# No chunk brought row by row, 311 counted chunks, three late node tiles, and other prices in the instruction planner of a two-layer graph kernel

## The chip, the core and the metric

The kernel runs on one core of a Trainium2 chip. TensorE (PE) multiplies matrices, VectorE (DVE) and ScalarE (ACT) work on elements, GpSimd (POOL) issues the indirect DMAs that gather rows by index, and SyncE (SP) issues most other DMAs; ScalarE issues some. The metric is the device time of one execution in microseconds. Differences below about 0.2% (2.5 us) are not told apart from no change.

## The reference

Two graph layers over N = 6250 nodes and E = 100000 edges sorted by target node `dst`, each an aggregation and a two-layer perceptron, then a residual layer norm (256 features in and out, 512 hidden):

```
def _gin_agg(h, src, dst, eps, n):
    return (1.0 + eps) * h + segment_sum(h[src], dst, n)
h = _gin_agg(x, src, dst, eps1, n)
h = relu(relu(h @ W1a + b1a) @ W1b + b1b)
h = _gin_agg(h, src, dst, eps2, n)
out = relu(h @ W2a + b2a) @ W2b + b2b
return layernorm(x + out)
# dst = min(6250 * uniform ** 2, 49999): low node numbers have many edges
```

The time goes into the two segment sums: 100000 rows of 256 floats in layer 1, 100000 rows of 512 floats in layer 2.

## The kernel before, in words

The nodes form 49 tiles of 128. The edges form 782 chunks of 128. A chunk's contribution to its targets is computed in one of two ways.

**Counted chunks** are the first 308, whose targets lie in the 8 heavy node tiles. For each chunk VectorE makes a one-hot of the source within its tile times all 49 tiles (`cb`, line 1923), ScalarE the one of the source's low part (`ca`, line 1902), PE multiplies them (line 1954) and VectorE adds the product into node-by-node counts (`upper_counts`, `lower_counts`, line 2181). The counts are used as a dense matrix: in layer 1 by `first_products` (line 1831), in layer 2 by `second_products` (line 1712), which multiplies the counts (`cf`, a float copy made by ScalarE at line 1639 of the bytes `ci` that SP loads at line 1621) with the layer-1 result of a range of nodes, split in two parts (`upper`, `xr`). The second products for the first ranges (those whose layer-1 nodes are done) run already in layer 1.

**Gathered chunks** are the others. GpSimd fetches 128 rows with one indirect DMA (line 527) into `early`, in layer 2 in turn with `late`, a tile in memory that layer 1 uses until its last second product. There is room for 24 gathers (PIECES = 6 pieces of BURST = 4). PE sums them by a one-hot of the targets (`sel`, line 1207), 2 pieces in a turn in layer 1 and 3 in layer 2; the sums are merged (lines 1258, 1262, 1278) and added by VectorE to the node tiles (line 1287).

A **dense block** then takes two node tiles: transposes (line 1331), first weights (line 1400), second weights (line 1433), and in layer 1 the bias and ReLU (lines 1446, 1449) and the store of `h1r` to DRAM (line 1450, on ScalarE's DMA queue); in layer 2 the layer norm and the output DMA (line 1496, on SP's). The layer-1 blocks of the last nodes end in the order of tiles ..., 11 and 10, 12, 9, 7, 8.

**Ferried chunks**: for five groups of layer 1 the group's last chunk isn't gathered by GpSimd. SP reads its 128 source indices into registers and issues 128 DMAs of one row (line 2217) into `b2b_c`, 640 in all, and one matmul for each (line 1219) sums it. When the last is summed `b2b_c` gets its own data, a bias (line 2221).

**Early gathers** (`fore`): gathers of layer 2 read the layer-1 result, so they wait for its stores. Two groups of 12 chunks each (FORES) go first and read only nodes below the LATE tiles (7 and 8), whose indices are replaced by a row of zeros; what the edges from the LATE tiles add comes later, by one-hot products of those tiles' own results: VectorE makes 24 one-hots over LATE's nodes (line 1113) and PE multiplies them.

Instructions are written in an order that is fixed before the kernel runs. A planner (class `Plan`) runs all steps as processes on a clock of its own, with a price in `yield ("on", engine, price, rank)`, rooms for the buffers, rests, and due times (GATHERS for a gather, LANDINGS, SUMS and TURN for the sums, PATIENT for the loads and casts of the ranges of the second products, HASTE for the layer-2 start). Its clock fixes only the order in each engine's queue; on the chip, semaphores decide when something runs. A different price therefore moves instructions in a queue without changing them.

Of the kernel before, what the change touches and what calls it, by code (L numbers as in the profile page):

```python
# [11 lines left out]
I32 = mybir.dt.int32  # L12
# [33 lines left out]
SIGMAS = 4.0  # L46
WIDTH = 4.5
# [44 lines left out]
def counted(N, E, tiles):  # L92
# [8 lines left out]
    while (  # L101
        node((total + PARTS) * P) < tiles * P
        and span(N, E, (total + PARTS) * P, P, SIGMAS) <= W
    ):
        total += PARTS
    k = -(-N // P)
    best = [(0.0, 0, 0)]
    for c in range(1, total + 1):
        found = []
        for n in range(1, min(c, LONGEST) + 1):  # L110
            w = min(math.ceil(span(N, E, c * P, n * P, WIDTH)), W)
            if span(N, E, c * P, n * P, SIGMAS) <= w:
# [87 lines left out]
GATHERS = (1.28, 1.265)  # L200
# [8 lines left out]
SUMS = 0.0021  # L209
TURN = (0.08, 0.2)  # L210
# [167 lines left out]
def tile_gin_residual_layernorm(  # L378
# [56 lines left out]
    NCP = groups[-1][0] + PARTS * groups[-1][1]  # L435
    runs = []
# [51 lines left out]
    ferries, t, free = [], FIRST, FERRY[0]  # L488
    for g in orders[1]:
        n = len(members[g])  # L490
        t += GATHERS[0] * n
        ready = free + FERRY[1] * P / FERRY[3] + FERRY[2]
        if ready <= t + LANDINGS[0] and t < FERRY[4] and members[g][-1][0] < full:
            ferries.append(g)
            t -= GATHERS[0]
            free = t + LANDINGS[0] + FERRY[2]
# [4 lines left out]
            for chunks in [members[g][: -1 if number == 1 and g in ferries else None]]  # L501
# [8 lines left out]
    fore = const.tile([P, FOREN], I32, name="fore")  # L510

# [35 lines left out]
    near = b1b_s = start = lowest = highest = ferried_from = None  # L547
# [280 lines left out]
    def ordered(ctx):  # L828
# [45 lines left out]
        def layer(number, pools, table, width, scale, weights, ba, wide, at=None, aside=None, right=None):  # L874
# [63 lines left out]
            sel_many = Tiles(keep, [P, GRP, SLOTS], F32, "sel", 2)  # L938
            to_room = Tiles(keep, [P, 2, P], F32R, "to", 4 if once else 5)
# [92 lines left out]
            def scaling(b, token):  # L1032
# [3 lines left out]
                yield ("on", "ACT", act(len(ts) * width), 2)  # L1036
# [42 lines left out]
            def late_edges(g):  # L1079
# [20 lines left out]
                assert len(hot) >= n  # L1100
# [10 lines left out]
                for i, (c, part) in enumerate(members[g]):  # L1111
                    yield ("on", "DVE", 0.22, 1)
                    nc.vector.tensor_scalar(
                        hot[i], numbers[:, : T * P], spot[:, c - c0 : c - c0 + 1], None,
                        op0=ALU.is_equal,
                    )
                assert n == PARTS * h
                yield ("on", "PE", 0.3 + 0.04 * n, 1)
                for i, (c, part) in enumerate(members[g]):
                    nc.tensor.matmul(  # L1120
                        ap[part * SLOTS : (part + 1) * SLOTS, : T * P], sel[:, c - c0, :], hot[i],
                        start=(i < PARTS), stop=(i >= n - PARTS),
                    )
# [50 lines left out]
            def sums():  # L1174
# [7 lines left out]
                while i < len(pieces[number]):  # L1182
# [4 lines left out]
                    for i in some:  # L1187
                        yield ("until", selected[pieces[number][i][0]])
                        yield ("until", arrived[i])
                        if once and i == last[pieces[1][i][0]] and pieces[1][i][0] in ferries:  # L1190
                            yield ("until", ferried[pieces[1][i][0]])
# [5 lines left out]
                    for i in some:  # L1197
# [18 lines left out]
                        if once and i == last[g] and g in ferries:  # L1216
# [3 lines left out]
                                pm[b * SLOTS : (b + 1) * SLOTS], sel[:, c - groups[g][0], :], b2b_c,  # L1220
# [21 lines left out]
            def merge(gs, shared):  # L1242
# [4 lines left out]
                yield ("on", "ACT", act(n * width), 0)  # L1247
# [35 lines left out]
                for i, (g, to, used, _) in enumerate(gs):  # L1283
                    for t in reach(g):
                        yield ("until", ready[t])
                        yield ("on", "DVE", dve(width), 1)
# [7 lines left out]
            def dense(b):  # L1294
# [98 lines left out]
                for o in range(0, KH, at_once):  # L1393
# [12 lines left out]
                    def hidden(token=token, fs=fs, todo=todo):  # L1406
                        for f in fs:
                            yield ("on", "ACT", act(nb), 1)
# [1149 lines left out]
```

## Time and profile before

| | before |
|---|---|
| median of 3 runs | 1265.28 us (1265.19 to 1265.89) |
| profiled execution | 1263.54 us, span 1261.8 us |
| mean granted TensorE clock | 0.974 |
| busy PE / DVE / ACT / POOL | 1173.7 (93%) / 832.2 (66%) / 653.5 (52%) / 908.6 (72%) us |
| gathers of layer 1, early ones, rest of layer 2 | 469, 24, 450 |

The profiled execution is 1.74 us longer than its span. POOL's busy 72% hides that an indirect DMA shows 0.95 us of work and 0.30 us of issue before the next one starts. L followed by a number is a line of the kernel before, and an engine's name with a q (ACTq, SPq) is its DMA issue. One matmul of 32-bit data in the program leaves two records on PE, so x16 in a PE row is 8 matmuls of the program.

### The profile page before, as it was taken

The page shows a single profiled execution, that of the slowest core. Times are in us where ns is not written, and L with a number is a line of the kernel's source. Part 1 is how long each engine was busy: PE and PEld are TensorE (multiplying, and loading weights), DVE is VectorE, ACT ScalarE, POOL GpSimd, SP SyncE. Part 2 cuts the span into 40 slices and gives each one's busy share as a digit, 9 for nine tenths or more (in the row PEclk, how much of TensorE's full clock was granted, in tenths as well). Part 3 has the DMA queues.
Part 4 walks back from the last instruction along what each step waited for, and adds up shares of the span by engine and source line. Part 5 has one row for each costly group of instructions (what it writes and reads, how often), then busy time and mean ns, then how long its engine had stood idle before and what let it go on. Part 6 is the DMA issues. An engine that isn't in the chain of part 4 may idle for free. (4 is left out here: it accounts for less than half of the span.)

```text
span 1261.8 us, 21174 instructions
## 1 busy us (share of the span) xinstructions
PE 1173.7 (93%) x6204; PEld 775.9 (61%) x6204; DVE 832.2 (66%) x2123; ACT 653.5 (52%) x1367; POOL 908.6 (72%) x956
## 2 busy tenths in 40 slices
PE   5879998999999999989979999998998999999998
PEld 4445455655555666556646767665766767777667
DVE  7899998888878743334356768676875565555243
ACT  7656678898896674534443633432533344321222
POOL 6777777777777777777267777777777777777760
PEclk9799999999999999989989999999998999999899
DMA  6445467666547776665388888888888888877871
GB/s 213 139 138 156 128 185 215 190 205 191 156 143 205 228 221 205 213 193 164 112 290 297 302 263 254 277 304 278 282 274 276 289 261 295 252 212 235 252 220 40
DMA packets 137652, 276.06 MB, mean 219 GB/s; under 512 B 21757, under 2 KB 68680, under 8 KB 137532
## 3 DMA queue, kind: packets, MB, share of 16 engines
q0 software_dynamic: 60432, 185.79, 48.0%
q1 hardware_dynamic: 43012, 56.43, 13.5%
q10 hardware_dynamic: 34088, 32.43, 8.0%
q8 instruction: 52, 0.85, 0.3%
q14 instruction: 68, 0.56, 0.2%
HBM read 248.95 MB, written 25.62 MB: 218 GB/s over the span
## 5 line engine op out<-in xcount | busy, mean ns | idle before, releaser
L527 POOL DMA_INDIRECT early<-in_x_dram,srcs x469 | 450.9, 961 | 146.3 <-issue 126.2
L527 POOL DMA_INDIRECT early<-h,places x226 | 216.4, 958 | 68.9 <-issue 54.5
L527 POOL DMA_INDIRECT late<-h,places x224 | 216.1, 965 | 68.2 <-issue 57.6
L1287 DVE SCALAR_TENSOR_TENSOR acc<-bank,mask,acc 128x256 f32<-128x256 f32 (+1 forms) x352 | 201.3, 603 | 59.1 <-PE bank L1278 57.2
L1433 PE MATMUL bank<-w1b_s,ht 128*128 128x512 f32 (+1 forms) x392 | 183.7, 595 | 0.4 <-ACT ht L1410 0.4
L1712 PE MATMUL bank<-upper,cf 128*128 128x512 f32 (+1 forms) x392 | 171.2, 437 | 8.7 <-ACT cf L1639 4.6
L1712 PE MATMUL bank<-xr,cf 128*128 128x512 f32 (+1 forms) x392 | 158.4, 404 | 2.7 <-DVE xr L1600 2.7
L1400 PE MATMUL bank<-zt,w2a_s 128*128 128x256 f32 (+2 forms) x736 | 152.0, 360 | 0.7 <-ACT zt L1359 0.7
L1400 PEld LDWEIGHTS bank<-zt,w2a_s 128*128 128x128 f32 x736 | 128.9, 192 | 25.5 <-issue 3.3
L1207 PE MATMUL bank<-early,sel 128*32 128x256 f32 (+1 forms) x1414 | 124.7, 467 | 18.9 <-DMA early<-h,places 6.2
L1639 ACT CAST cf<-ci 128x512 fp32r<-128x512 uint8 (+1 forms) x104 | 60.9, 594 | 154.3 <-PE bank L1712 113.5
L1657 DVE TENSOR_TENSOR whole_acc<-bank,whole_acc 128x512 f32<-128x512 f32 x96 | 65.1, 683 | 86.0 <-PE bank L1712 86.0
L1061 DVE TENSOR_TENSOR sel<-iota,slot 128x256 f32<-128x256 f32 (+2 forms) x112 | 49.0, 437 | 95.6 <-PE bank L1207 91.9
L1831 PE MATMUL bank<-cf,xh 128*128 128x512 f32 x392 | 108.8, 418 | 1.7 <-DVE xh L1770 1.5
L1902 ACT ACTIVATE ca<-numbers,low 128x128 f16<-128x128 f16 x308 | 98.1, 391 | 21.8 <-PE bank L1954 20.0
L1433 PEld LDWEIGHTS bank<-w1b_s,ht 128*128 128x128 f32 (+1 forms) x392 | 71.6, 190 | 60.6 <-issue 52.9
L1278 PE MATMUL bank<-split,to 128*128 128x512 f32 (+2 forms) x332 | 92.4, 397 | 15.4 <-ACT split L1258 7.6
L1410 ACT ACTIVATE ht<-bank,b2a_s 128x256 f32<-128x256 f32 (+2 forms) x92 | 37.1, 446 | 130.4 <-PE bank L1400 130.4
L1400 PE MATMUL bank<-zt,w1a_s 128*128 128x256 f32 (+2 forms) x432 | 97.2, 371 | 4.8 <-ACT zt L1359 3.8
L1258 ACT CAST split<-bank 128x512 fp32r<-128x512 f32 (+1 forms) x111 | 63.6, 583 | 66.3 <-PE bank L1207 53.1
L1712 PEld LDWEIGHTS bank<-upper,cf 128*128 128x128 f32 (+1 forms) x392 | 75.3, 192 | 33.1 <-ACT upper L1595 5.8
L1207 PEld LDWEIGHTS bank<-early,sel 128*32 128x32 f32 x1414 | 38.3, 110 | 91.1 <-issue 45.5
(203 smaller groups left out, 1870.6 us busy)
## 6 DMA issues: line engine op xcount, KB each, us to landing
raw<-in_x_dram ACTq DMA_DIRECT2D x48, 256.0 KB
h<-h1r ACTq DMA_DIRECT2D x48, 256.0 KB
b2b_c<-in_x_dram SPq DMA_DIRECT2D x640, 1.0 KB
xr<-h SPq DMA_DIRECT2D x10, 1024.0 KB
acc<-h SPq DMA_DIRECT2D x17, 512.0 KB
early<-in_x_dram,srcs POOLq DMA_INDIRECT x469
ci<-counts SPq DMA_DIRECT2D x24, 256.0 KB
acc<-in_x_dram SPq DMA_DIRECT2D x21, 256.0 KB
```

Of the source, the lines that this page charges most:

```text
L527: nc.gpsimd.indirect_dma_start(out=rows_[:, j, :], out_offset=None, in_=table, in_offset=bass.IndirectOffsetOnAxis(ap=rows_in[:, c - first ...
L1207: mm = nc.tensor.matmul(pm[b * SLOTS : (b + 1) * SLOTS], sel[:, c - groups[g][0], :], rows_[:, l, :], start=(c == part[0]), stop=(c == par ...
L1258: nc.scalar.copy(to_ if parted else to_.bitcast(F32), ap[:used, at_])
L1278: nc.tensor.matmul(pu[:, at_], lhs, rhs, start=(l == 0), stop=(l == 1 or not parted),)
L1287: nc.vector.scalar_tensor_tensor(acc[t], pu[:, i * width : (i + 1) * width], mask[:, t - lo[g], g : g + 1], acc[t], op0=ALU.mult, op1=ALU.add,
L1400: nc.tensor.matmul(ph[:, (f - o) * TILES * P : (f - o) * TILES * P + nb], wa[:, k, f * P : (f + 1) * P], zt[:, k, :nb], start=(k == 0), st ...
L1433: nc.tensor.matmul(po[:m], ht[:, f, i * P : i * P + m], wb[:, f, :], start=(f == 0), stop=(f == KH - 1),)
L1639: nc.scalar.copy(cf_token.tile[:, : n * P].rearrange("p (k j) -> p k j", j=P), token.tile[:, :n, a : a + P],)
L1657: nc.vector.tensor_tensor(sums_of[t], bank[token.number][:, :width], sums_of[t], op=ALU.add)
L1712: nc.tensor.matmul(bank[token.number][:, :width], cf[:m, j * P : (j + 1) * P], of[:m, j, :], start=(j == 0 and of is upper), stop=(j == le ...
L1831: nc.tensor.matmul(bank[tokens[f].number][:, :c], xh[:m, j, l, f * P : (f + 1) * P], cf[:m, :c], start=(k == 0 and l == 0), stop=(k == NT ...
L1902: nc.scalar.activation(token.tile[:, j, :], numbers[:, :P], AF.Abs, bias=low[:, q * BATCH + j : q * BATCH + j + 1],)
```

## The change

No chunk is ferried any more in layer 1; the code can now ferry in layer 2 too, but the limits in FERRY (-10 and -90) let no group through in either layer. The number of counted chunks no longer rises in steps of PARTS and may exceed the window's width by OVER = 0.1, which makes it 311. So layer 1 has 471 gathers (469 before: 5 ferried ones come back, 3 become counted) and layer 2 has 24 early and 447 others (450). LATE covers tiles 7 to 9, so the one-hots of the early groups' late part are 384 wide (256 before) and are made in two halves; FORES becomes the next lower two groups, over two node tiles that are set `apart` instead of three. A number of prices and due times is changed. The rest of the diff changes the code of ferrying, for rows that are not used here.

```
-PATIENT = 16.0
+PATIENT = (16.0, 16.0, 9.0)
-FERRY = (45.0, 5.6, 5.0, 8, 610.0)
+FERRY = ((45.0, 0.7, 5.0, -10.0, 1), (4.0, 0.52, 6.0, -90.0, 1))
-LATE = (7, 9)
-HASTE = -20.0
+LATE = (7, 10)
+HASTE = -23.0
...
-    while (
-        node((total + PARTS) * P) < tiles * P
-        and span(N, E, (total + PARTS) * P, P, SIGMAS) <= W
-    ):
-        total += PARTS
+    while node((total + 1) * P) < tiles * P and span(N, E, (total + 1) * P, P, SIGMAS) < W + OVER:
+        total += 1
...
-GATHERS = (1.28, 1.265)
+GATHERS = (1.262, 1.262)
...
-SUMS = 0.0021
-TURN = (0.08, 0.2)
+SUMS = 0.00168
+TURN = (0.12, 0.12)
...
+                for o in range(0, n, turn_):
+                    some = list(enumerate(members[g]))[o : o + turn_]
+                    for i, (c, part) in some:
+                        yield ("on", "DVE", 0.1 + 0.0005 * T * P, 1)
+                        nc.vector.tensor_scalar(
+                            hot[i - o], numbers[:, : T * P], spot[:, c - c0 : c - c0 + 1], None,
+                            op0=ALU.is_equal,
+                        )
...
-                    yield ("on", "PE", 0.14 * kk * len(some), 2)
+                    yield ("on", "PE", 0.11 * kk * len(some), 2)
...
-                            yield ("on", "DVE", (2 if soon else 3) * dve(D) + 0.2, 2)
+                            yield ("on", "DVE", (1.03 if soon else 1.49), 2)
...
-                            yield ("on", "PE", 2 * PASS * len(ks) * width, first or 3)
+                            yield ("on", "PE", 0.2 + 2 * PASS * len(ks) * width, first or 3)
...
-                            cost += 0.16 + 0.00027 * NT * width_of[c]
+                            cost += 0.125 + 0.00027 * NT * width_of[c]
...
-                yield ("on", "DVE", 0.2 + 0.00106 * NT * w, 1)
+                yield ("on", "DVE", 0.08 + 0.00106 * NT * w, 1)
...
-                nc.sync.dma_start(b2b_c, b2b.partition_broadcast(P))
...
+                if once:
+                    for i in range(len(mine), len(ferries[2])):
+                        edges_in(from2, 2, i)
+                    for g in mine:
+                        yield ("until", landed[g])
+                    nc.sync.dma_start(b2b_c, b2b.partition_broadcast(P))
```

SP's queue late in layer 1, before. A row is a line, what is issued and its shape; `b2b_c` is the ferry's tile, `ferried_from` its indices, `ci_8014` the count bytes of one half of the heavy tiles for a range, `xr` that range's layer-1 result.

```order
L2217 DMA b2b_c<-in_x_dram 1x256
L1621 DMA ci_8014<-counts 128x2048
L2211 TENSOR_LOAD ferried_from
L2217 ISA
...
L1518 DMA xr<-h_60 128x4x512
L1621 DMA ci_8107<-counts 128x2048
L1621 DMA ci_8178<-counts 128x2048
L1518 DMA xr<-h_60 128x4x512
L2221 DMA b2b_c<-in_L_gnn_b2b_dram 128x256
```

The same place after the change:

```order
L1529 DMA acc_5744<-h_60 128x2x512
L1634 DMA ci_5782<-counts 128x2048
L1529 DMA acc_5800<-h_60 128x2x512
L1634 DMA ci_6002<-counts 128x2048
L1529 DMA xr<-h_60 128x4x512
L1634 DMA ci_6076<-counts 128x2048
L1634 DMA ci_6160<-counts 128x2048
```

Ahead of and behind each load of count bytes there were row loads of the ferry; now only other loads of the second products and of the seeds stand there.

GpSimd's gathers at the seam of the two layers, before:

```order
L527 DMA early<-in_x_dram,srcs 128x256 x469
L527 DMA early<-h_60,fore 128x512 x12
L527 DMA late<-h_60,fore 128x512 x12
L527 DMA early<-h_60,places_72 128x512 x10
```

After the change:

```order
L535 DMA early<-in_x_dram,srcs 128x256 x471
L535 DMA early<-h_60,fore 128x512 x12
L535 DMA late<-h_60,fore 128x512 x12
L535 DMA early<-h_60,places_72 128x512 x11
```

Two gathers more stand ahead of the early ones; the order and number of the early ones are the same.

TensorE from the last sum of layer 2 (line 1207 before, 1217 after) on, before:

```order
L1207 MATMUL bank_95<-late,sel 32x512 x4
L1433 MATMUL bank_92<-w2b_s,ht 128x256 x2
L1400 MATMUL bank_98<-zt,w2a_s 128x128 x8
L1278 MATMUL bank_91<-split,to 128x512 x2
...
L1331 MATMUL bank_94<-ident,whole_acc 128x128 x4
L1433 MATMUL bank_93<-w2b_s,ht 128x256 x2
L1331 MATMUL bank_97<-ident,apart 128x128 x4
L1400 MATMUL bank_95<-xr,w2a_s 128x128 x8
L1433 MATMUL bank_93<-w2b_s,ht 128x256 x2
```

After the change:

```order
L1217 MATMUL bank_98<-late,sel 32x512 x4
L1444 MATMUL bank_97<-w2b_s,ht 128x256 x2
L1342 MATMUL bank_99<-ident,acc_10424 128x128 x4
L1289 MATMUL bank_93<-split,to 128x512 x2
L1411 MATMUL bank_95<-zt,w2a_s 128x128 x8
L1342 MATMUL bank_96<-ident,whole_acc 128x128 x4
L1411 MATMUL bank_94<-zt,w2a_s 128x128 x8
L1342 MATMUL bank_92<-ident,apart 128x128 x4
L1411 MATMUL bank_98<-xr,w2a_s 128x128 x8
```

Behind the last sum to the end stand, before, 8 blocks of first weights (8 matmuls each), 10 of second weights (2 each), 12 transposes and 2 merge matmuls; after, 6, 7, 12 and 2.

## Rows read from the trace of the kernel before

**Rows 1.** Timeline of POOL: start, length, engine, line, tile, count, idle before and releaser.
```profile
599.09 0.94 POOL L527 DMA_INDIRECT early<-in_x_dram,srcs  x1 [0.30 <-issue]
...
621.27 0.94 POOL L527 DMA_INDIRECT early<-h,fore  x1 [21.24 <-PE bank L1400]
...
640.69 1.33 POOL L527 DMA_INDIRECT late<-h,fore  x1 [4.72 <-issue]
...
656.16 0.95 POOL L527 DMA_INDIRECT early<-h,places  x1 [0.30 <-PE bank L1207]
...
1224.34 1.12 POOL L527 DMA_INDIRECT late<-h,places  x1 [0.30 <-issue]
```

**Rows 2.** Groups of POOL: count, busy us, mean ns, idle before and its releasers.
```profile
L527 POOL DMA_INDIRECT early<-h,places x226 | 216.4, 958 | 68.9 <-issue 54.5 <-DMA early<-h,places 6.1 <-DMA late<-h,places 1.8
L527 POOL DMA_INDIRECT late<-h,places x224 | 216.1, 965 | 68.2 <-issue 57.6 <-DMA late<-h,places 5.2 <-PE bank L1712 1.5
```

**Rows 3.** Busy time in two stretches: PE, PEld, DVE, ACT, POOL, clock, DMA.
```profile
100.00:150.00 50.00, 44.44 (x227) 25.44 (x226) 46.43 (x120) 31.79 (x75) 38.11 (x40) 0.97 0.49 148
600.00:640.00 40.00, 38.87 (x189) 26.53 (x187) 12.58 (x22) 15.15 (x29) 11.38 (x13) 1.00 0.42 136
```

**Rows 4.** Timeline of ACT's DMA queue and PE at the seam.
```profile
601.74 0.33 ACTq L1450 DMA_DIRECT2D h<-h1r  x1
...
617.39 0.33 ACTq L1450 DMA_DIRECT2D h<-h1r  x1
...
633.76 0.39 PE L1712 MATMUL bank<-upper,cf 128*128 128x512 f32 x1
...
639.56 0.39 PE L1712 MATMUL bank<-xr,cf 128*128 128x512 f32 x1
```

**Rows 5.** Timeline of SP's queue, ACT and PE around 554 us.
```profile
523.88 26.47 SPq L2217 DMA_DIRECT2D b2b_c<-in_x_dram  x40
...
532.89 0.30 ACT L1639 CAST cf<-ci 128x128 fp32r<-128x128 uint8 x1 [1.62 <-PE bank L1712]
...
550.45 0.36 SPq L1621 DMA_DIRECT2D ci<-counts  x1
...
553.92 2.17 ACT L1639 CAST cf<-ci 128x512 fp32r<-128x512 uint8 x4 [10.85 <-DMA ci<-counts]
...
554.60 0.79 PE L1712 MATMUL bank<-upper,cf 128*128 128x512 f32 x1 [4.55 <-ACT cf L1639]
```

**Rows 6.** Groups of VectorE at the widest count step.
```profile
L2181 DVE TENSOR_TENSOR upper_counts<-bank,upper_counts 128x490 f32 x45 | 29.6, 659 | 2.4 <-PE bank L1954 1.9
L1923 DVE TENSOR_SCALAR cb<-numbers,si 128x490 f16<-128x490 f16 x78 | 25.6, 367 | 1.1 <-PE bank L1954 1.1
```

**Rows 7.** Timeline of VectorE and POOL at the late one-hots.
```profile
659.50 3.30 DVE L1113 TENSOR_SCALAR ht<-numbers,zt 128x256 f16<-128x256 f16 x16
...
662.61 1.02 POOL L527 DMA_INDIRECT early<-h,places  x1 [0.30 <-issue]
```

**Rows 8.** Timeline of PE from the last sum to the end.
```profile
1229.66 1.07 PE L1207 MATMUL bank<-late,sel 128*32 128x512 f32 x8 [1.76 <-DMA late<-h,places]
...
1242.69 1.95 PE L1400 MATMUL bank<-xr,w2a_s 128*128 128x128 f32 x16
1244.48 1.95 PE L1400 MATMUL bank<-zt,w2a_s 128*128 128x128 f32 x16
...
1253.73 1.89 PE L1433 MATMUL bank<-w2b_s,ht 128*128 128x256 f32 x8
```

**Rows 9.** Waits of PE from 640 us on: total us, times, longest.
```profile
PE bank L1207 <- DMA late<-h,places: 7.0, 3, 3.0
PE bank L1207 <- DMA early<-h,places: 6.2, 4, 4.1
```

**Rows 10.** Timeline of POOL and PE: a turn's first gather, and its sum.
```profile
1064.43 0.95 POOL L527 DMA_INDIRECT late<-h,places  x1 [0.30 <-PE bank L1712]
...
1081.94 2.78 PE L1207 MATMUL bank<-late,sel 128*32 128x512 f32 x24
```

More of the change, by code (lines that the diff above doesn't have):

```diff
@@ L435, in tile_gin_residual_layernorm @@
     NCP = groups[-1][0] + PARTS * groups[-1][1]
+    MOST = max(h for c, h in groups) * PARTS
     runs = []
@@ L487, in tile_gin_residual_layernorm @@
     orders[2] = FORES + [g for g in reversed(range(BEGIN[1], NG)) if g not in FORES]
[L488 to L496, printed above, removed]
+    ferries = {}
+    for number, order in orders.items():
+        begin, pace, landing, until, rooms_ = FERRY[number - 1]
+        t, sp, free, found = (FIRST, HASTE)[number - 1], begin, [begin] * rooms_, []
+        for g in order:
+            t += GATHERS[number - 1] * len(members[g])
+            ready = max(sp, free[len(found) % rooms_]) + pace * P + landing
+            if (
+                ready <= t + LANDINGS[number - 1] and t < until and members[g][-1][0] < full
+                and (number == 1 or g not in FORES)
+            ):
+                t -= GATHERS[number - 1]
+                sp = ready - landing
+                free[len(found) % rooms_] = t + LANDINGS[number - 1] + landing
+                found.append(g)
+        ferries[number] = found
     pieces = {
@@ L500, in tile_gin_residual_layernorm @@
             for g in order
-            for chunks in [members[g][: -1 if number == 1 and g in ferries else None]]
+            for chunks in [members[g][: -1 if g in ferries[number] else None]]
             for i in range(0, len(chunks), BURST)
@@ L546, in tile_gin_residual_layernorm @@
     flag = const.tile([1, 1], I32, name="flag")
-    near = b1b_s = start = lowest = highest = ferried_from = None
+    near = b1b_s = start = lowest = highest = ferried_from = ferried_to = None
     e1 = const.tile([P, 2], F32, name="e1")
@@ L1110, in late_edges @@
                 ap = bank[token.number]
[L1111 to L1116, printed above, removed]
-                assert n == PARTS * h
[L1118 to L1123, printed above, removed]
+                assert n == PARTS * h
+                for o in range(0, n, turn_):
[6 more added lines that the diff above has]
+                        )
+                    yield ("on", "PE", 0.2 + 0.0002 * T * P * len(some), 1)
+                    for i, (c, part) in some:
+                        nc.tensor.matmul(
+                            ap[part * SLOTS : (part + 1) * SLOTS, : T * P], sel[:, c - c0, :],
+                            hot[i - o], start=(i < PARTS), stop=(i >= n - PARTS),
+                        )
                 flat = b[:, : 2 * T * P].bitcast(F32)
@@ L1189, in sums @@
                         yield ("until", arrived[i])
-                        if once and i == last[pieces[1][i][0]] and pieces[1][i][0] in ferries:
-                            yield ("until", ferried[pieces[1][i][0]])
+                        if i == last[pieces[number][i][0]] and pieces[number][i][0] in ferried:
+                            yield ("until", ferried[pieces[number][i][0]])
                     for i in some:
@@ L1215, in sums @@
                         last_sum[i] = mm
-                        if once and i == last[g] and g in ferries:
+                        if i == last[g] and g in ferried:
                             c, b = members[g][-1]
@@ L1549, in second_products @@
                 if not once:
-                    sown_room = sown["room"] = Tiles(leave, [P, TILES, width], F32, "sown", 1)
+                    sown_room = sown["room"] = Tiles(
+                        leave, [P, max(TILES, LATE[1] - LATE[0]), width], F32, "sown", 1
+                    )
                 halved = {r: Event(plan) for r in rs}
@@ L1973, in placing, with moved @@
                 most = NT * W // 2
-                to_late = GAP + 1 - LATE[0] * P
+                def moved(to, of, above):
+                    nc.vector.tensor_scalar(
+                        above, of, float(LATE[0] * P), float(GAP + 1 - LATE[0] * P),
+                        op0=ALU.is_ge, op1=ALU.mult,
+                    )
+                    nc.vector.tensor_tensor(above, above, of, op=ALU.add)
+                    nc.vector.tensor_scalar(
+                        to, of, float(LATE[1] * P), float(N + 1 - LATE[0] * P),
+                        op0=ALU.is_ge, op1=ALU.mult,
+                    )
+                    nc.vector.tensor_tensor(to, above, to, op=ALU.subtract)
                 for a in range(NC2, NCP, most):
@@ L2253, in layer @@
                 plan.start(selecting())
+                plan.start(ferrying())
                 plan.ending = HASTE
@@ L2269, in ordered @@
             )
-            nonlocal near, b1b_s, start, lowest, highest, ferried_from
+            nonlocal near, b1b_s, start, lowest, highest, ferried_from, ferried_to
             near = first.tile([P, NC], F32, name="near")
-            ferried_from = first.tile([1, 2 * P], I32, name="ferried_from")
+            ferried_from = first.tile([max(len(ferries[1]), 1), P], I32, name="ferried_from")
+            ferried_to = [b2b_c] + [
+                first.tile([P, D], F32, name=f"ferried{i}") for i in range(1, FERRY[0][4])
+            ]
             b1b_s = first.tile([P, H], F32, name="b1b_s")
```

95 lines of the change are left out of this document (53 added, 42 removed).

## The prediction

> **What bounds the kernel now.** I read the timeline of GpSimd first, since an aggregation is paced by its gathers. One gather follows the other 1.25 us apart, and only two pauses stand out [rows 1]: 21.24 us ahead of the first early gather at 621.27 and 4.72 us ahead of the second dozen at 640.69. From 656.16 to 1224.34 there is none: 450 gathers (226 + 224 in [rows 2]) lie 568.18 / 449 = 1.2654 us apart, and their idle time is the 0.30 us of issue that each shows, whatever releaser is named. So from about 640 on the kernel runs at GpSimd's pace, and the end is the last gather plus a tail.
>
> The seam comes next, in the timeline of the other engines. The early gathers start 3.88 us after the store of a layer-1 tile was issued at 617.39 [rows 1, 4]; by the order of stores it is that of tile 9, the last that is not LATE. The second dozen goes into `late`, memory that layer 1 uses until its last second product. That matmul starts at 639.56 and ends at 639.95 [rows 4], and the gather starts 0.74 us later. I call 639.95 the gate. It is a gate of TensorE: PE is busy for 38.87 of the 40 us from 600 to 640 [rows 3], so what moves it is work and idle time of PE before it. One piece of idle time stands out: 4.55 us at 554.60, a second product that waits for `cf`, whose ScalarE cast waits 10.85 us for the bytes `ci` [rows 5]. Their load is issued only at 550.45, behind 40 row loads of the ferry that fill SP's queue from 523.88 to 550.35. The previous cast of single-tile bytes had ended by 533.19, so no reader held that load back for the last 17 us.
>
> Last the tail: after the last gather (1224.34) the last sum starts at 1229.66, PE then works without a pause until 1253.73 + 1.89 = 1255.62 [rows 1, 8], and 6.2 us of norm and output DMA close the span of 1261.8.
>
> **The change part by part.**
>
> Ferry removed. The 640 row loads go, and in the new order no load of `ci` stands behind a row. The 4.55 us of PE go [rows 5]. Below, nothing is gained if PE next waits for something else at that place (0); above, the ScalarE wait of 10.85 us bounds it. I take 4.55, since PE is at 38.87 of 40 afterwards and would fill the hole with work it has to do before the gate anyway. The five chunks come back as gathers, three others become counted: 471 for 469. That is 2 x 1.25 = 2.5 us of GpSimd ahead of the early gathers, covered by the 21.24 us pause. The ten matmuls of the ferry become ten of sums.
>
> Three more counted chunks. Each costs VectorE 0.367 + 0.659 = 1.03 us [rows 6], together 3.1. From 100 to 150 us, VectorE is busy 46.43 and PE 44.44 of 50 [rows 3]: neither alone bounds that stretch. Ends: 0 (hidden) and +3.1 (all of it). I take +1.0 on the gate, nearer to the hidden end because the stretch has 3.6 us left on VectorE.
>
> Gate: 639.95 - 4.55 + 1.0 = 636.4.
>
> LATE covers tile 9. The early gathers now wait for tile 12's store, issued at 601.74 in the run of before [rows 4]; with 3.88 us that is 605.6, so they start between 602 and 612, not at 621. That is about 14 us sooner and I count it as **nothing**: the first dozen then ends sooner, but the second dozen still waits for the gate, and the pause of 21 us is moved from before the first dozen to before the second. Below it could cost 1 us, if stores lie later; above it gains only the sum of the first dozen, which can now run ahead of the gate: 2.78 us, as a sum of 12 gathers takes [rows 10]. 24 one-hots get wider by half: 16 of them now take 3.30 us [rows 7], 0.206 each, so 24 x 0.206 x 0.5 = 2.5 us more of VectorE, which has room there. While those ran, a gather took 1.02 instead of 0.95 us [rows 7]: 0.07. I take 0. The Trainium skill (SBUF — State Buffer, "Who interferes with whom") says that VectorE in its two-port modes, which such compares can enter, holds a port pair that it shares with GpSimd, and whoever comes second is blocked for the whole instruction. By that rule the wider one-hots could push the gathers back by up to 2.5 us; the trace shows far less, 0.07 for the gather among them.
>
> Three fewer gathers in layer 2: 471 for 474, of which 447 behind the early ones for 450: -3 x 1.2654 = -3.8.
>
> Last gather: 1224.34 - (639.95 - 636.4) - 3.8 = 1217.0.
>
> Tail. Behind the last sum the order has 6 blocks of first weights for 8 and 7 of second weights for 10. A block of the first kind takes 1244.48 - 1242.69 = 1.79 us, one of the second about 1.89 / 2 = 0.9 [rows 8]: -(2 x 1.79 + 3 x 0.9) = -6.3. That work went ahead of the sum, where PE waited 13.2 us in all for gathered rows [rows 9], so it fits there. But with less filling the last chain of sum, merge, add, transpose, copy, weights stands closer together, and PE may wait in it: between 0 and 6.3 (all lost). I take +1.5, about the length of one such wait, as the 1.76 us ahead of the last sum [rows 8].
>
> Sum: last gather 1217.0, + 5.3 to the last sum (1229.66 - 1224.34), + 26.0 to the end of PE (1255.62 - 1229.66), - 6.3 + 1.5, + 6.2 to the end of the span = 1249.7, 12.1 below 1261.8. The profiled execution is 1.74 us above its span, and the median shown (1265.28) another 1.74 above that execution: 1253.2. A thousand places in the queues move through the new prices, and each can make an engine wait for another; I add 0.8 for it: **1254.0**.
>
> Prices and due times. The rest of the change adds no instruction; it moves them. In the new order PE has more work ahead of the same sums: ahead of the sum of layer 2's 24th gather 16 more matmuls of the second product, ahead of that of its 240th 32 more. From 633.76 to 639.56 there are 26 of them [rows 4], 0.23 us each, so 3.7 and 7.4 us. A turn's sum runs 1081.94 - 1064.43 = 17.5 us after its first gather is issued [rows 10], and with room for 24 gathers GpSimd waits from 24 x 1.2654 = 30.4 us on. 17.5 + 7.4 = 24.9 stays below, so I count 0; from 12.9 us of more work ahead of a sum on it would cost.
>
> **The rivals.**
>
> A, half of it. PE's sums come so late that GpSimd waits for buffers, or the gate doesn't move since another wait takes the place of the `cf` one. For it: the 13.2 us of waits for rows are the slack that the earlier work is to fill, and dense blocks pulled ahead add to the lag. Against: 5 us are left to the ceiling. Time: 1254.0 + 4.55 (the gate) + 2.4 (half of the tail's net 4.8) = 1261.
>
> B, no change. The gate doesn't move and the whole net 4.8 us of the tail are lost: 1254.0 + 4.55 + 4.8 = 1263.4, up to 1266 with one more wait like those in [rows 9]. For it: only the three gathers (3.8) are sure. Against: the row that shows the 4.55 us wait names its cause.
>
> C, slower. In the new order PE has 99 counted chunks ahead of the sum of layer 1's 100th gather, not 84. If VectorE can't make them as early, PE stops in front of each and the sums behind it, the gathers' buffers, and with them the gate are late: 15 x 1.03 = 15.4 us, 1253.0 + 15.4 = 1268.4. It decides from 14.6 us on (1267.8 against 1253.2). For it: 46.43 of 50 us busy on VectorE [rows 3]. Against: GpSimd's 21 us pause takes up a late gather, and later in layer 1 counting comes to an end sooner by the same 15 chunks.
>
> D, more. If GpSimd's pace stops being the limit, only PE is left: 1261.8 - 13.2 (its waits for rows in layer 2) - 4.55 = 1244, 1247.5 as a median. It would need gathers faster than 1.2654, which the change doesn't give; 1247 if the gate comes 5 us sooner still through better packed layer 1.
>
> **How the numbers follow.** Forecast, 1249 to 1257: 0.5. A, 1257 to 1263: 0.2. B: 0.08. C: 0.12. D, below 1249: 0.1. The range is 1246 to 1266: it leaves out C and the lower part of D. 0.2% (2.5 us) is about what a measurement of this kernel can tell from no change: faster than 1262.8 is the forecast, D and A, 0.8; within it B, 0.08; slower C, 0.12.
>
> **What would show it.** Right: no row loads, no PE wait for `cf` near 550; first early gather between 602 and 612, a pause of 10 to 20 us ahead of the second dozen, which starts near 637; the last gather near 1217; PE's waits for rows in layer 2 below 13.2 us; 20 to 21.5 us from the last sum to the end of PE instead of 26.0. Wrong: the second dozen at 640 or later (A, C), pauses of GpSimd over 1 us after the seam (A), waits of PE for `cb` or for counts in the first 200 us (C), a gather spacing other than 1.265 (D, or the port rule if wider only near the one-hots).

## The result, and the profile after

| | before | after |
|---|---|---|
| median | 1264.37 us (1259.25 to 1268.57, 16 runs) | 1256.77 us (1252.02 to 1261.41, 16 runs) |
| ratio, 95% interval | | 0.9942 (0.9927 to 0.9957) |
| span of the profiled execution | 1261.8 us | 1256.1 us |
| mean granted TensorE clock | 0.974 | 0.980 |

The change makes the kernel 7.6 us faster, 0.58%, inside the range and with the sign that was forecast; the forecast was 11.3 us. The two profiled executions differ by 5.7 us, and the steps below are told by those two.

The timeline of GpSimd after, at the places of [rows 1]:

```profile
602.87 0.94 POOL L535 DMA_INDIRECT early<-in_x_dram,srcs  x1 [0.30 <-issue]
610.09 0.95 POOL L535 DMA_INDIRECT early<-h,fore  x1 [6.27 <-issue]
...
638.17 0.95 POOL L535 DMA_INDIRECT late<-h,fore  x1 [13.34 <-issue]
...
653.21 0.95 POOL L535 DMA_INDIRECT early<-h,places  x1 [0.31 <-issue]
...
1218.76 0.95 POOL L535 DMA_INDIRECT late<-h,places  x1 [0.30 <-issue]
```

The first dozen of early gathers starts 11.2 us sooner, and the pause ahead of the second dozen has grown from 4.72 to 13.34 us. The first later gather comes 2.95 us sooner and the last 5.58. From the last gather to the end of the span it is 37.3 us for 37.5 before: of the 5.7 us, 2.95 come at the seam, 2.63 between the first later gather and the last, and 0.1 behind it.

TensorE at the seam after, which answers to the second half of [rows 4]: the last second weights of layer 1, then second products, the last of them, and the first sum of layer 2.

```profile
624.79 7.03 PE L1444 MATMUL bank<-w1b_s,ht 128*128 128x512 f32 x16
631.26 0.80 PE L1725 MATMUL bank<-upper,cf 128*128 128x512 f32 x1
...
637.03 0.40 PE L1725 MATMUL bank<-xr,cf 128*128 128x512 f32 x1
638.86 2.78 PE L1217 MATMUL bank<-early,sel 128*32 128x512 f32 x24 [1.43 <-issue]
```

The gate is at 637.43, 2.5 us sooner than 639.95, and the second dozen starts 0.74 us behind it in both kernels. Between the last dense block and the gate stand 24 second-product matmuls, 6.2 us; the order of before has 48 there. (A second product leaves one record, not two as other matmuls of 32-bit data do: the profile counts 2 x 392 for 8 heavy tiles x 49 tiles of nodes x 2 parts.)

TensorE from the last sum to the end, which answers to [rows 8]:

```profile
1224.67 1.07 PE L1217 MATMUL bank<-late,sel 128*32 128x512 f32 x8
...
1227.96 2.05 PE L1411 MATMUL bank<-zt,w2a_s 128*128 128x128 f32 x16 [0.27 <-ACT zt L1370]
1232.33 0.66 PE L1342 MATMUL bank<-ident,whole_acc 128*128 128x128 f32 x4 [2.32 <-DVE whole_acc L1298]
1232.83 3.24 PE L1411 MATMUL bank<-zt,w2a_s 128*128 128x128 f32 x16
...
1248.15 1.03 PE L1444 MATMUL bank<-w2b_s,ht 128*128 128x256 f32 x4
```

From the last sum to the end of PE it is 24.5 us (1249.18 - 1224.67) for 26.0. Two blocks of first weights and three of second weights are gone, but PE waits 2.32 us for the adds into `whole_acc`, and the block behind that wait takes 3.24 us where others take 1.95. The last sum also starts 5.9 us behind the last gather instead of 5.3, and the norm and the output take 6.9 us instead of 6.2.

PE's longest waits from 640 us on, in total, times and longest. Of the 13.2 us for gathered rows in [rows 9] the 3.8 us of the last line are left; the first two lines have grown, from 0.7 and 1.4 us:

```profile
PE bank L1342 <- DVE acc L1298: 5.2, 3, 4.1
PE bank L1217 <- issue: 3.9, 4, 1.5
PE bank L1217 <- DMA late<-h,places: 3.8, 3, 2.5
```

### The profile page after: what moved, and what is told of

It is laid out like the page before. It is cut to its first block, busy times and chain, and to the rows that moved or that the text cites. A ratio compares the mean times of both kernels' runs of the same rounds, so it can differ in the third digit from the quotient of the medians.

```text
span 1256.1 us, 19100 instructions
## 1 busy us (share of the span) xinstructions
PE 1174.6 (94%) x6201; PEld 777.0 (62%) x6201; DVE 834.9 (66%) x2116; ACT 657.8 (52%) x1371; POOL 909.6 (72%) x955
## 3 DMA queue, kind: packets, MB, share of 16 engines
q1 hardware_dynamic: 41850, 56.03, 13.2%
## 5 line engine op out<-in xcount | busy, mean ns | idle before, releaser
L535 POOL DMA_INDIRECT early<-h,places x227 | 219.5, 967 | 69.2 <-issue 59.4
L535 POOL DMA_INDIRECT late<-h,places x220 | 211.1, 959 | 67.1 <-issue 56.7
L1411 PE MATMUL bank<-zt,w2a_s 128*128 128x256 f32 (+2 forms) x736 | 154.8, 366 | 0.9 <-ACT zt L1370 0.9
L1273 DVE TENSOR_TENSOR split<-bank,split 128x512 fp32r<-128x512 f32 (+1 forms) x111 | 73.1, 682 | 33.6 <-ACT split L1269 33.4
L1936 DVE TENSOR_SCALAR cb<-numbers,si 128x490 f16<-128x490 f16 (+8 forms) x311 | 91.0, 337 | 5.6 <-PE bank L1967 5.4
```

The lines of the kernel that those rows point to most:

```text
L535: nc.gpsimd.indirect_dma_start(out=rows_[:, j, :], out_offset=None, in_=table, in_offset=bass.IndirectOffsetOnAxis(ap=rows_in[:, c - first ...
L1273: nc.vector.tensor_tensor(split[:used, 1, at_], ap[:used, at_], split[:used, 0, at_], op=ALU.subtract,)
L1411: nc.tensor.matmul(ph[:, (f - o) * TILES * P : (f - o) * TILES * P + nb], wa[:, k, f * P : (f + 1) * P], zt[:, k, :nb], start=(k == 0), st ...
L1936: made = nc.vector.tensor_scalar(token.tile[:, : NT * width_of[c]], numbers[:, : NT * width_of[c]], spot[:, c : c + 1], None, op0=ALU.is_e ...
```

## The experiments

e1 to e4, e8 to e10 and e11 ran on three chips on which every kernel took 1561 to 1607 us: the kernel before took 1607 us beside e1 to e4, 1603 beside e8 to e10, 1607 beside e11. All engines sit idle there for stretches that end in no event of the kernel. Sizes are therefore taken only from e5, e6, e7 and e12, beside which the kernel before took 1262.3 to 1263.9 us. The trace of e6 is of its longest execution (1259.1 us, median 1257.1), that of e7 of its shortest (1244.7, median 1247.3), so where two traces are compared, some 2 us are no difference of the kernels.

Ratios are to the kernel before on the same chip, with 95% intervals.

| run | kernel | ratio |
|---|---|---|
| e5 | before, no ferry | 0.9993 (0.9982 to 1.0005) |
| e6 | before, no ferry, new prices | 0.9946 (0.9926 to 0.9966) |
| | after | 0.9942 (0.9927 to 0.9957) |
| e7 | after, 308 counted chunks | 0.9878 (0.9854 to 0.9903) |
| e12 | after, GATHERS as before in layer 1 | 0.9871 (0.9848 to 0.9895) |
| e1 | as e5, slower chip | 0.9767 (0.9729 to 0.9805) |
| e2 | as e6, slower chip | 0.9998 (0.9959 to 1.0037) |
| e3 | as e7, slower chip | 0.9988 (0.9951 to 1.0025) |
| e4 | after, LATE of two tiles, slower chip | 0.9873 (0.9841 to 0.9905) |
| e8, e11 | as e12, slower chips | 0.9816 (0.9765 to 0.9868), 0.9880 (0.9834 to 0.9926) |
| e9 | as e12, LATE of two tiles, slower chip | 0.9922 (0.9883 to 0.9960) |
| e10 | as e4, slower chip | 0.9816 (0.9760 to 0.9873) |

**The ferry alone (e1, e5).**

```diff
-FERRY = (45.0, 5.6, 5.0, 8, 610.0)
+FERRY = (45.0, 5.6, 5.0, 8, -10.0)
```

Expected of e1: 

> The kernel before, with the ferry switched off and nothing else: the five chunks come back as gathers of layer 1, 308 chunks stay counted, all old prices stay. Theory (the ferry's row loads held back a load of ci, and the 4.55 us of PE lay on the path to the gate): no PE wait for cf near 550, the last second product of layer 1 ends near 635.5 to 637.5 instead of 639.95, the time is 3 to 4.5 us lower, about 1260 against 1264.4. Rival (PE's hole is only refilled elsewhere, and the gain of the change comes from prices and from the three counted chunks): gate at 639 to 640, time 1264.

Expected of e5: 

> The kernel of e1 once more, since the kernel before took 1607 us beside e1 to e4 and 1264 us elsewhere: PE, VectorE, ScalarE and GpSimd all show idle time of several us there that ends in no event of the kernel. If the kernel before is near 1264 us here: theory (the ferry's row loads held back ci, 4.55 us of PE on the path to the gate): gate at 635.5 to 637.5, time 3 to 4.5 us lower, about 1260. Rival (the hole is refilled elsewhere): gate 639 to 640, time 1264. If it is again near 1600: then idle time without an event decides, and the ratio should again be near 0.977.

Measured in e5: 1261.1 us against 1262.7, a ratio that holds no change. The wait for `cf` is gone (no wait of PE over 1 us from 430 to 637 us), and the gate moves, by 2.0 us:

```profile
637.50 0.40 PE L1712 MATMUL bank<-xr,cf 128*128 128x512 f32 x1
639.33 1.92 PE L1207 MATMUL bank<-early,sel 128*32 128x512 f32 x16 [1.43 <-issue]
```

Of the 4.55 us less than half reaches the gate; PE idles more earlier on, 12.1 us between 150 and 300 us, where the kernel before idles 8.3. Of those 2.0 us the time shows 0.9, between 2.3 gained and 0.6 lost. The gate lies between the two forecasts, nearer to the theory's (635.5 to 637.5); the time is the rival's.

**The prices on top (e2, e6).** The kernel of e5 with all new prices of single steps, of GATHERS, SUMS and TURN, among them:

```diff
-GATHERS = (1.28, 1.265)
+GATHERS = (1.262, 1.262)
-SUMS = 0.0021
-TURN = (0.08, 0.2)
+SUMS = 0.00168
+TURN = (0.12, 0.12)
```

Expected of e2: 

> The kernel before without the ferry and with the new prices of the planner (GATHERS, SUMS, TURN and the prices of single steps), but with 308 counted chunks, LATE of two tiles, the old due times. Theory (prices only move work from behind the last sum to ahead of it, and what they do to counting is hidden): gate as without the ferry alone, 24 to 25 us from the last sum to the end of PE instead of 26, 1 to 2 us faster than without the ferry alone, about 1258.5. Rival (prices that pull 14 counted chunks ahead of layer 1's 100th sum make PE wait for cb, 6.5 us instead of 2.0): gate 2 to 4 us later than without the ferry alone, time about 1262.

Expected of e6: 

> The kernel of e2 once more: the kernel before without the ferry (e5) and with the new prices, 308 counted chunks, LATE of two tiles, the old due times. In e5 the gate came 2.0 us sooner (637.9) and the time was 0.1% lower. Theory (prices put dense blocks ahead of the last sum that stood behind it, and that is worth 1 to 4 us; what they do to counting is hidden): gate 636.5 to 638.5, 22 to 25 us from the last sum to the end of PE instead of 26.0, time 2 to 4 us below e5, ratio 0.996 to 0.998. Rival (prices that pull 14 counted chunks ahead of layer 1's 100th sum make PE wait for cb, and the gate comes 2 to 4 us later than in e5): ratio 0.999 to 1.002.

Measured in e6: 1257.1 us against 1262.3, about all that the whole change gives. GpSimd in e6, first early gather, second dozen, first later gather and last:

```profile
626.69 0.95 POOL L527 DMA_INDIRECT early<-h,fore  x1 [18.37 <-PE bank L1400]
...
641.72 0.95 POOL L527 DMA_INDIRECT late<-h,fore  x1 [0.30 <-issue]
...
657.37 1.01 POOL L527 DMA_INDIRECT early<-h,places  x1 [0.30 <-issue]
...
1224.45 0.95 POOL L527 DMA_INDIRECT late<-h,places  x1 [0.30 <-issue]
```

The last gather is where that of before is (1224.34), and 3.5 us behind that of e5 (1220.97). PE in e6, its last second product of layer 1:

```profile
635.18 0.40 PE L1712 MATMUL bank<-xr,cf 128*128 128x512 f32 x1
```

Only 8 second products stand behind the last dense block here (32 in e5), and the gate is at 635.58. The second dozen doesn't wait for it: it follows the first without a pause. But the dense blocks come later for it, tile 9's store is issued at 623.53 instead of 619.05, and the first dozen, which waits for that store, starts 4.0 us behind that of e5 (622.67). So the prices take the gate out of the way and lose at the first dozen what that could give. What is shorter lies behind the last gather. PE at the end of e6, last sum and last block:

```profile
1228.06 1.06 PE L1207 MATMUL bank<-late,sel 128*32 128x512 f32 x8
...
1249.38 1.03 PE L1433 MATMUL bank<-w2b_s,ht 128*128 128x256 f32 x4
```

The last sum comes 3.6 us after the last gather (5.3 before) and PE ends 22.4 us after that sum (26.0 before): 5.3 us. The theory holds for the tail and, above its upper end, for the time; what it left out is the seam. PE did wait longer for `cb` (5.3 us in layer 1, 2.0 before), but the gate is sooner than in e5, not later as the rival has it.

**308 counted chunks (e3, e7).**

```diff
-    while node((total + 1) * P) < tiles * P and span(N, E, (total + 1) * P, P, SIGMAS) < W + OVER:
-        total += 1
+    while node((total + PARTS) * P) < tiles * P and span(N, E, (total + PARTS) * P, P, SIGMAS) <= W:
+        total += PARTS
```

Expected of e3: 

> The changed kernel with 308 counted chunks, as before: three gathers more in each layer (474 in layer 1, 474 in layer 2). Theory (after the gate each gather is 1.266 us of the end): 3.8 us later from the gate to the last gather, less at most 1 us of earlier gate, so 1259.5 to 1260.5 against 1256.8. Rival (the three counted chunks cost VectorE and with it the gate about what they save): the gate 2.5 to 4 us earlier than with 311, time 1256.8.

Expected of e7: 

> The kernel of e3 once more: the changed kernel with 308 counted chunks, so three gathers more in each layer. Theory (after the gate each gather is 1.266 us of the end): 3.8 us from the gate to the last gather, less up to 1 us of earlier gate: 3 to 4 us slower than the changed kernel, ratio to the kernel before 0.9965 to 0.9975 where the changed kernel has 0.9942. Rival (three more counted chunks cost the gate what they save): gate 2.5 to 4 us sooner than 637.4, ratio 0.994.

Measured in e7: 1247.3 us against 1262.3. With three gathers more in each layer it is not 3.8 us slower than the changed kernel but some 8 us faster (0.9878 against 0.9942). Neither theory had that. GpSimd in e7:

```profile
607.82 0.94 POOL L535 DMA_INDIRECT early<-h,fore  x1 [1.05 <-PE bank L1289]
...
624.43 0.95 POOL L535 DMA_INDIRECT late<-h,fore  x1 [0.30 <-issue]
...
640.73 0.95 POOL L535 DMA_INDIRECT early<-h,places  x1 [1.26 <-issue]
...
1209.63 0.95 POOL L535 DMA_INDIRECT late<-h,places  x1 [0.30 <-issue]
```

The second dozen follows the first without a pause: the gate is gone. PE of e7 shows why. Its last second product of layer 1 and its last second weights:

```profile
613.92 0.40 PE L1725 MATMUL bank<-xr,cf 128*128 128x512 f32 x1
...
626.88 7.03 PE L1444 MATMUL bank<-w1b_s,ht 128*128 128x512 f32 x16
...
635.20 2.78 PE L1217 MATMUL bank<-early,sel 128*32 128x512 f32 x24 [1.29 <-issue]
```

PE reaches layer 2 at 635.20, 3.7 us sooner than in the changed kernel (638.86). But all 208 second-product matmuls of layer 1 stand ahead of its last dense blocks, so the memory that `late` takes over is free at 614 instead of 637, 23 us sooner.

**The place of the last second product, with 311 counted chunks (e8, e11, e12).** One number of the changed kernel makes the planner's order of e7 there, too: none behind the last dense block.

```diff
-GATHERS = (1.262, 1.262)
+GATHERS = (1.28, 1.262)
```

Expected of e8: 

> The changed kernel with one number as before: the planner's price of a gather in layer 1 is 1.28 again (1.262 in the change); 311 counted chunks, no ferry, LATE of three tiles and all other prices as changed. In the order it gives, none of layer 1's 208 second-product matmuls stands behind the last second-weight block of layer 1; in the changed kernel 24 of them do, in the one of e7 none. Theory (the memory of late comes free with the last second product of layer 1, so where that stands in PE's order decides; the pause ahead of the second dozen is gone if it stands ahead of the last dense blocks): the second dozen starts right behind the first, near 622 to 625, the first of the later gathers near 641 instead of 653, the last gather near 1205 (three gathers or 3.8 us sooner than e7's 1209.6), the time 1241 to 1246, ratio 0.983 to 0.987. Rival (e7 is faster since 308 chunks are counted, not 311; the three cost VectorE and PE in the first 200 us more than they save): the time stays at 1253 to 1257, ratio 0.993 to 0.995.

Expected of e11: 

> The kernel of e8 once more, since the kernel before took 1603 us beside e8 to e10. If the kernel before is near 1263 us here: theory (the place of the last second product of layer 1 in PE's order decides when the second dozen starts): the second dozen starts right behind the first, near 622 to 625, the first of the later gathers near 641, the last gather near 1205, the time 1241 to 1246, ratio 0.983 to 0.987. Rival (e7 was faster since 308 chunks are counted, not 311): 1253 to 1257, ratio 0.993 to 0.995.

Expected of e12: 

> The kernel of e8 and e11 a third time, since the kernel before took 1603 to 1607 us beside those. If the kernel before is near 1263 us here: theory (the place of the last second product of layer 1 in PE's order decides when the second dozen starts): the second dozen starts right behind the first, near 622 to 625, the first of the later gathers near 641, the last gather near 1205, the time 1241 to 1246, ratio 0.983 to 0.987. Rival (e7 was faster since 308 chunks are counted, not 311): 1253 to 1257, ratio 0.993 to 0.995. If it is near 1600 again: the second dozen 0.30 us behind the first, as in e8, and a wait of some 10 us ahead of the first later gather.

Measured in e12: 1248.8 us against 1263.9. The interval doesn't meet that of the changed kernel, and is that of e7. So the three counted chunks are not what slowed the changed kernel by 8 us. The price moves other steps of layer 1, too; that the place of 24 matmuls counts is read from the trace. GpSimd in e12:

```profile
614.58 0.94 POOL L535 DMA_INDIRECT early<-h,fore  x1 [6.84 <-PE bank L1342]
...
630.58 0.95 POOL L535 DMA_INDIRECT late<-h,fore  x1 [0.30 <-issue]
...
646.59 0.94 POOL L535 DMA_INDIRECT early<-h,places  x1 [0.89 <-issue]
...
1206.79 0.95 POOL L535 DMA_INDIRECT late<-h,places  x1 [0.30 <-issue]
```

And its PE, with the last second product, the last second weights and the last sum:

```profile
615.86 0.39 PE L1725 MATMUL bank<-xr,cf 128*128 128x512 f32 x1
...
630.97 7.03 PE L1444 MATMUL bank<-w1b_s,ht 128*128 128x512 f32 x16
...
1218.36 1.07 PE L1217 MATMUL bank<-late,sel 128*32 128x512 f32 x8
```

The second dozen starts at 630.58, 5.6 us or more later than I expected, and the ratio ends just above the range named. That start is 7.6 us sooner than in the changed kernel, the first later gather 6.6. The last gather is at 1206.79, 12.0 us sooner, 5.4 of them from gathers closer together; the last sum only 6.3 us sooner. It starts 11.6 us after the last gather instead of 5.9, and in e12 no wait of PE that the profile puts down to gathered rows is left from 640 us on: PE has become the limit behind the gate, busy 551.66 of the 567 us from 640 to 1207. That fits with three gathers fewer than e7 bringing nothing (0.9871 against 0.9878), though two intervals of some 3 us to either side can't tell 3.8 us from nothing for certain. The spans of e12 and the changed kernel differ by 8.9 us: 6.3 lie ahead of the last sum, 2.6 behind it, where e12 has no wait of 2.32 us and no slow block; those aren't the seam's.

On the slower chips the gathers come in the same order. GpSimd in e8, last of the first dozen, first of the second, first later gather:

```profile
802.37 0.95 POOL L535 DMA_INDIRECT early<-h,fore  x1 [0.30 <-issue]
803.62 0.94 POOL L535 DMA_INDIRECT late<-h,fore  x1 [0.30 <-issue]
...
829.01 0.95 POOL L535 DMA_INDIRECT early<-h,places  x1 [10.65 <-PE bank L1217]
```

There the later gathers wait for a sum of PE instead, 10.65 us. e1, e4 and e10, whose orders have 24 second products or more behind the last dense block, pause 3.1 to 3.3 us at the second dozen, e2, e3, e8, e9 and e11 not.

**LATE of two tiles (e4, e9, e10).** In e4 and e10 the changed kernel, in e9 the kernel of e12:

```diff
-LATE = (7, 10)
-HASTE = -23.0
+LATE = (7, 9)
+HASTE = -20.0
```

Expected of e4: 

> The changed kernel with LATE over tiles 7 and 8 and HASTE -20, as before: the early gathers wait for the store of tile 9. Theory (the second dozen waits for the gate in any case, so the earlier start of the first is worth nothing): the first early gather near 624 instead of 610, the second dozen near 638 as in the changed kernel, the time 1256 to 1257.5, the same as with three late tiles. Rival (the earlier start counts): the second dozen or the first of the later gathers 3 us or more behind the changed kernel's 638.2 and 653.2, time 1260 or more.

Expected of e9: 

> The kernel of e8 with LATE over tiles 7 and 8 and HASTE -20, as before. Up to layer 1's 470th sum PE's order is that of e8. Theory (once the second dozen no longer waits for a second product, the first dozen's start decides, and that is the store of the last tile that is not LATE): the first early gather near 620 instead of 608, the first of the later gathers near 651, the time 8 to 12 us above e8, 1251 to 1256. Rival (the third late tile is worth nothing, as the prediction counted it): the same as e8 within 3 us.

Expected of e10: 

> The kernel of e4 once more: the changed kernel with LATE over tiles 7 and 8 and HASTE -20, with 24 second-product matmuls behind layer 1's last dense block, as in the changed kernel. Theory (with the second dozen waiting for those, the start of the first is worth nothing): the first early gather near 622, the second dozen near 638, the first of the later gathers near 653, the time as the changed kernel's, ratio 0.993 to 0.996. Rival (the start of the first dozen counts here too): the first of the later gathers at 656 or later, ratio 0.997 to 1.000.

All three ran on slower chips, so none of the times named can be compared. On one chip e9 was 1.1% slower than e8, as the theory has it for an order without the gate, but e10 was level with e8, where the theory wants it slower by 1%. The place of the second products doesn't decide on such a chip.

What the early start is worth shows in e6 and e7. They ran on one chip, both with 308 counted chunks, no ferry and the same prices of gathers and sums, and in both the second dozen follows the first without a pause. Between them lie the third late tile with its HASTE and FORES, PATIENT, and smaller parts of the change. The first dozen starts at 607.82 in e7 and at 626.69 in e6, the last gather is 14.8 us sooner, and the ratio falls from 0.9946 to 0.9878, 8.6 us, with intervals that don't meet. In the changed kernel the gate takes it back: 11.2 us at the first dozen, then the pause of 13.34. On the slower chip of e2 and e3, the same two kernels, the times are level (0.9998 and 0.9988).

## Why the prediction was right, and for which wrong reasons

**The total** was right within its range, 1256.8 for 1254.0 (1246 to 1266). The signs of the seam came, too: the first early gather at 610.09 (602 to 612), a pause of 13.34 us (10 to 20), the second dozen at 638.17 (near 637). The split was not right, and part of the fit is luck. The sum gave a span of 1249.7 us, measured were 1256.1, 6.4 more: 1.8 at the last gather, 0.6 up to the last sum, 3.3 from there to the end of PE and 0.7 behind it. The 4.3 us that the sum adds from span to median were 0.7, which takes 3.6 back.

**Ferry.** Forecast -4.55 at the gate and at the end. The wait and the row loads did go, but e5 shows 2.0 us at the gate and 0.9 us (2.3 to -0.6) in time. The step that failed is "PE ... would fill the hole with work it has to do before the gate anyway": one wait went and idle time elsewhere, earlier, grew.

**Gate as an amount of work.** "It is a gate of TensorE ... so what moves it is work and idle time of PE before it" was true of the time at which PE ends layer 1, and wrong for `late`. Its memory is bound to one matmul, the last second product, and the planner's order sets where that stands. By moving it ahead of the dense blocks, e12 starts the second dozen 7.6 us before the changed kernel does, though its PE comes to layer 2 later (639.30 for 638.86). The prediction counted the early start as "nothing" because of the gate, and that holds while the gate comes behind the end of the first dozen: after the change 24 matmuls stand behind the last dense block, 6.2 us, and the second dozen waits for them. Without the gate the early start counts, 8.6 us between e6 and e7. And without the early start a gate out of the way is worth nothing at the seam: e6's second dozen starts at 641.72, behind that of the kernel before (640.69). That the prices could take the gate out of the way was seen by none of the rivals.

**Prices.** "Adds no instruction; it moves them ... I count 0" was said of everything but the tail. e6 shows what they move: 3.5 us lost at the seam against e5, 4.7 won from the last gather to the end of PE (5.3 against the kernel before), and a ratio 0.0047 under e5's, about 5.9 us, where the traces show 2.0.

**Tail.** It was given -6.3 + 1.5 = -4.8, as a part of the change and not of the prices. Mechanism and size hold for e6. In the changed kernel itself this step failed: from the last sum to the end of PE it is 24.5 us for the 21.2 forecast, and from the last gather to the end of the span 0.1 is won. Of the 3.3 missing, 1.1 are waits (2.32 + 0.27 for the 1.5 taken) and 1.7 the slower block and transposes behind the wait (3.24 for 1.95 and 1.00 for 0.60 us); 0.5 stay open.

**Three counted chunks.** -3.8 for three gathers: the last gather does come 2.63 us sooner beyond the 2.95 of the first (5.58 in all), with the gathers 1.2681 us apart instead of 1.2654, which took 1.2 back (446 x 0.0027). As time they can't be told: between e7 and e12 the ratios differ by 0.0007. The 1.0 us on the gate that I took for them stays open: PE comes to layer 2 at 639.30 in e12 and at 635.20 in e7, but the orders of the two differ by more than these chunks.

**Rival C** (counting moved ahead, VectorE the bound) had its sign: PE waited 6.5 us for `cb` in layer 1 instead of 2.0. It was far from the 14.6 us from which it decides. (Its 1268.4 starts from 1253.0, where the sum gives 1253.2 or, with the last term, 1254.0.) **Rival A** named 1261, and the measured 1256.8 lies between the forecast and it, at the upper end of the forecast's own 1249 to 1257; part of its reason came, since idle time elsewhere took half of the place of the `cf` wait, and half of the tail's gain or more was lost. **Rival D**, PE as the bound, is what e12 runs into; it named 1247.5, and e7 and e12 took 1247.3 and 1248.8, though not by faster gathers as D wanted but by an earlier start of them.

**Port rule.** The 24 wider one-hots took 6.28 us (4.95 before), 1.33 more where 2.5 was forecast. The gathers beside them took up to 1.30 us; over the four slowed ones that is 0.69 us above 0.95 each, for 0.33 over three before. The Trainium skill (SBUF — State Buffer, "Who interferes with whom") says that of a VectorE instruction in a two-port mode and one of GpSimd the second is blocked until the first is done. The trace has such a delay, but only 0.36 us more of it than before, a seventh of the 2.5 us that the prediction named.

**What stays open:** why idle time of PE from 150 to 300 us grew when the ferry went; what the third late tile is worth by itself, without PATIENT and HASTE; why the time shows 5.9 us between e5 and e6 and the traces 2.0; and what holds all engines back on the slower chips.

## What to carry to other kernels

A buffer that took over another's memory waited here for one instruction, not for an amount of work: its first use came 0.74 us after that instruction in the kernels before and after and in e5. When a pause ends with "the memory is free", look up which instruction frees it and what stands ahead of that one in its queue, before counting how busy the engine is. Then look at what the move pushes back: with three late tiles, second products ahead of the last dense blocks went with 8 us less time, as much as the whole change brings; with two, the blocks that came later held the store for which the first gathers wait (e6), and the seam gained nothing. In a kernel whose order comes from prices, a change of 1.4% in one price can move such an instruction; count what stands behind it in the new order each time.

## What the runs showed of the hardware

The pace of the gathers differs a little between runs: 1.2681 us in the changed kernel, 1.2654 in the one before, 1.2670 in e7, 1.2561 in e12. The changed kernel and e12 have the same 447; over them the ends are 5.4 us apart, nearly as much as this change brings. It is the gathers themselves that differ, not the 0.30 us between them: they are busy 430.6 us in the one and 425.3 in the other. What lengthens single ones stays open, but for those beside the one-hots.

Behind PE's 2.32 us wait in the tail the granted clock of the stretch from 1232 to 1236 us was 0.66, against 1.00 from 1224 to 1232; part of it ran at the lower of the two levels, 1.2 GHz, and the block there took 3.24 instead of 1.95 us. So this wait cost nearly twice its length. It needn't: e7 has a longer one in its tail, behind which the clock stayed at 1.00 (1217 to 1224 us) and the next block took 1.95 us.

```profile
1219.97 0.50 PE L1289 MATMUL bank<-split,to 128*128 128x512 f32 x1 [2.98 <-DVE split L1273]
```

On three chips the kernel before took 1603 to 1607 us. In e1, on one of them, PE waits in 39 places ahead of one line, for instance, with no event behind it:

```profile
PE bank L1207 <- issue: 39.6, 39, 4.4
```

No run here shows where that comes from. The ranking of kernels is another there (e1, without the ferry alone, is the fastest of e1 to e4), so a gain of half a per cent on one chip says little of another.
